# Tile finishing in a transformer layer with experts: from a fixed place in each tile step to stages placed by the list scheduler

## The chip, the cores and the metric

The kernel runs on one core of a Trainium2 chip. The metric is the device time of one execution in microseconds (us), taken as the median of several runs. A core has five engines that run beside each other, each with its own queue that it works through in order: PE (TensorE, matrix products), DVE (VectorE, elementwise work and reductions), ACT (ScalarE, activations and copies), POOL (GpSimd; here it issues the indirect transfers and takes inverse square roots) and SP (SyncE, plain transfers). An instruction that waits holds up everything behind it in its queue.

## The reference

The input x has 4 sequences of 1024 tokens with 256 channels. The first half of the layer is causal attention with 16 heads and a slope per head. The second half is a small attention over the four tokens of one position, followed by a choice of one of eight experts for each token and two layers of that expert. Cut to what matters here:

```python
h = _layernorm(x + attn_out, ln1_g, ln1_b)
flat = h.reshape(-1, C)
logits = flat @ router_w.T + router_b
probs = jax.nn.softmax(logits, axis=-1)
_, top_i = jax.lax.top_k(probs, 2)
assign = jnp.max(top_i, axis=-1)
for e in range(E):
    he = jax.nn.gelu(flat @ w1[e].T + b1[e], approximate=False)
    oe = he @ w2[e].T + b2[e]
    out = jnp.where((assign == e)[:, None], oe, out)
return _layernorm(h + moe_out, ln2_g, ln2_b)
```

So each token goes through one expert only, and x is added to what is returned.

## The kernel before

**The first 660 us** are the causal attention, with "fronts" laid between its products. A front (`front`) handles one block of 128 positions of all four sequences: normalisation, the small attention (`pr` and `sc` are scores, `pv` weighted values), the output projection `ao` with its residual, the normalisation h (root `rstd_h`, then `shift_h` and four ACT instructions that apply it), the choice of the expert (`key`, `before`, `equal`, `rank`, `hot`) and the place of each token among those of its expert (`counts_all`, `place`). It stores two rows for each token in HBM: h, and x with the last shift added.

**Tiles.** Tokens of one expert are gathered into tiles of 128. A table says which rows belong to a tile. The first table (18 tiles, 0 to 17) is made from the first six fronts, the second (20 tiles, again numbered from 0) when the last front has counted (`tabulate_rest`, lines 1228 to 1264, the product `who` at line 1314). A tile passes through these steps:

- `gather` (line 1733): an indirect transfer on POOL brings the 128 rows into one of 18 buffers `given`.
- `stages`, step 1 (line 1776): PE transposes h into the PSUM tile `t` (`mtp`; one buffer), ACT copies it (`mt`); ACT also copies the expert's first weights (line 1766).
- step 2 (line 1792): PE makes `hid`, ACT applies Gelu (`ge`, line 1801).
- step 3 (line 1811): PE makes `oe`, two tiles to a PSUM bank. With `by_product` (all of the first table, the last two of the second) PE also adds h (line 1819), else DVE does it later (line 1828) and so frees the bank early.
- finishing (`finish_tiles`): DVE takes mean and variance (lines 730, 731, 735), POOL the inverse root (`norm_root`, line 745), DVE makes the output `o` in two instructions (lines 1838 and 1841; four buffers), POOL writes a one-column clearing (`spare`, line 1848) and issues the scattered write (line 1849).

One `advance` moves each tile under way by one step, so that PE runs transposes of tile k+2, `hid` of k+1 and `oe` of k behind each other. In the old kernel `advance` begins with `finish`: finishing goes in pairs, and each tile step lets each pair under way take one more step (statistics and root; then `o`; then the output).

**The order around the change** is written out by a small list scheduler at build time (from line 2180). `threads` holds the stages of the last fronts; `free` holds when each engine is planned to be free; each stage says on which engine it is heavy and for how long; the stage that can begin first is written out next. Where PE would be free more than `TILE_HALF` (1.3 planned us) before the next stage, a tile step is written instead (`tile_step`), with the costs of `TILE`. Five tiles are held back to cover the second table. Then `late["wide"]` is set, attention's PSUM banks (`bank`, three) serve `oe` too beside its own three, and tile steps follow until nothing is left:

```python
    while experts.left():
        tile_step()
        n += 1
        if n == 8:
            check_sums()
```

`check_sums` tests whether the softmax sums are in range; its product `n_badp` and `odd` (line 2244) decide whether a general program runs behind this one.

Of the kernel before, what the change touches and what calls it, by code (L numbers as in the profile page):

```python
# [37 lines left out]
P = 128  # L38
# [30 lines left out]

TILE = (("PE", 2.6), ("DVE", 1.7), ("ACT", 1.9), ("POOL", 2.3))  # L70
TILE_HALF, LAG, COPIED, FIRST_BY, W1_THERE, LOAD_W2 = 1.3, 0.2, 1.0, 0.1, 22.0, 10.0
# [503 lines left out]
def fast_layer(ctx: ExitStack, tc: tile.TileContext, odd, x, wq, wk, wv, wp, w_in, w_out, w_r,  # L575
# [78 lines left out]
    def row(at, n=C):  # L654
        return row_sb[:, at - G1:at - G1 + n]
# [82 lines left out]
    def norm_stats(src, n, name, tag=""):  # L738
        tiles = norm_tiles(name, tag)
        for i in range(n):  # L740
            norm_one(tiles, i, src(i))
        return norm_end(tiles, n)
# [980 lines left out]
    class Tile:  # L1723
# [46 lines left out]
        def stages(self):  # L1770
# [32 lines left out]
            if late["n_oe"] % 2 == 0:  # L1803
                if late["wide"] and late["n_oe"] % 4:
                    late["oe"] = bank(f"oe_{name}").rearrange("p (k c) -> p k c", c=C)
                else:
                    late["oe"] = ps.tile([P, 2, C], F32, tag="o", name=f"oe_{name}", bufs=3)
# [14 lines left out]
    def finish_tiles(two):  # L1822

        n, name = len(two), two[0].name
        for t in two:
            if not t.by_product:
                own = t.hx[:, :C]
                nc.vector.tensor_tensor(own, own, t.v, ALU.add)
                t.v = own
        mv, rstd = norm_stats(lambda k: two[k].v, n, f"v_{name}", "_v")  # L1830
        norm_root(rstd, n)
        yield
        if experts.waiting():
            yield
        os = []
        for k, t in enumerate(two):
            o = late["work"].tile([P, C], F32, tag="o", name=f"o_{t.name}", bufs=4)
            nc.vector.scalar_tensor_tensor(  # L1838
                o, t.v, mv[:, k, 0:1], row(G2), ALU.subtract, ALU.mult
            )  # L1840
            nc.vector.scalar_tensor_tensor(  # L1841
                o, o, rstd[:, k:k + 1], t.hx[:, C:2 * C], ALU.mult, ALU.add
            )
            os.append(o)
        if experts.waiting():
            yield
        for t, o in zip(two, os):
            nc.gpsimd.memset(spare, 0.0)  # L1848
            ins = nc.gpsimd.indirect_dma_start(  # L1849
                out=out.rearrange("t n c -> (t n) c"),  # L1850
                out_offset=bass.IndirectOffsetOnAxis(ap=t.table.out_rows[:, t.j:t.j + 1], axis=0),
                in_=o, in_offset=None, bounds_check=B * T - 1, oob_is_err=False,
            )
            if late["n_out"]:
                tc.declare_no_dep(ins.ins, group="rows", reason="a token is in one tile")
            tc.add_to_no_dep_group("rows", ins.ins)
            late["n_out"] += 1

    class Experts:
# [3 lines left out]
        def __init__(self):  # L1863
            self.step, self.fetched = 0, []
            self.n_fetched = self.n_finished = 0
            self.under_way, self.done, self.finishing = [], [], []

        def fetch(self):
            self.step += 1
            if tiles_to_do and self.n_fetched - self.n_finished < len(given):  # L1870
                t = tiles_to_do.pop(0)
                t.by_product = t.table.n == 0 or len(tiles_to_do) < 2
                t.gather(given[self.n_fetched % len(given)])
                if self.n_fetched < N_OWN:
                    t.load_weights()
                self.n_fetched += 1
                self.fetched.append((t, self.step))

        def finish(self):
            for it in list(self.finishing):  # L1880
                n, stages = it
                if next(stages, self) is self:
                    self.finishing.remove(it)
                    self.n_finished += n
            n = 1 if self.done and len(self.done) + len(self.under_way) + self.waiting() < 3 else 2
            if len(self.done) >= n:
                two, self.done = self.done[:n], self.done[n:]
                self.finishing.append((len(two), finish_tiles(two)))
                next(self.finishing[-1][1])

        def waiting(self):
            return len(tiles_to_do) + len(self.fetched)

        def left(self):
            return (len(tiles_to_do) + len(self.fetched)
                    + len(self.under_way) + len(self.done) + len(self.finishing))

        def advance(self, finish=True):
            if finish:
                self.finish()  # L1900


            last = []
            if self.fetched and self.fetched[0][1] <= self.step - 3:
                t, _ = self.fetched.pop(0)
                last = [(t, t.stages())]
            if self.fetched and self.n_fetched > 2 * N_OWN + 1:
                t, _ = self.fetched[0]
                if not t.w1:
                    t.copy_w1()  # L1910
            for it in last + self.under_way[::-1]:
                t, stages = it
                if next(stages, self) is self:
                    self.under_way.remove(it)
                    self.done.append(t)
            self.under_way += last

    experts = Experts()
# [216 lines left out]
    def load_layer(sb, src):  # L2135
# [3 lines left out]
    late.update(  # L2139
        tail=tail, work=work, ps=ps_x, wide=False, n_oe=0, n_out=0, n_hid=0,  # L2140
        w1=w1_sb.rearrange("p e c f -> p (e c f)"), w2=w2_sb.rearrange("p e c f -> p (e c f)"),
# [40 lines left out]
    threads[0].ready = 9.0  # L2182
    engine_of = {"E": "DVE", "P": "DVE", "A": "ACT", "N": "ACT", "R": "POOL", "D": "PE", "d": "PE"}

# [5 lines left out]
    def take(it, at):  # L2190
# [10 lines left out]
        if it.kind == "end":  # L2201
            threads.remove(it)

    def tile_begin():
        return max(free["PE"], W1_THERE if experts.n_fetched > 2 * N_OWN else 0.0)

    def tile_step(finish=True):
        at = tile_begin()
        for on, cost in TILE:
            if on != "DVE" or experts.finishing or len(experts.done) == 2:  # L2210
                free[on] = max(free[on], at) + cost
        experts.fetch()
        experts.advance(finish)

    while threads:
        for at, what in list(of_late):
            if free["PE"] >= at:
                of_late.remove((at, what))
                what()
        at, _, it = min((begin(it) + FIRST_BY * n, n, it) for n, it in enumerate(threads))  # L2220
        if (
# [5 lines left out]
    for _ in range(HELD_BACK // 2):  # L2227
        tile_step(False)
    for _ in part.tabulate_rest():
        pass  # L2230
    late["n_oe"] += late["n_oe"] % 2
    late["wide"] = True
    for _ in range(2):
        experts.fetch()
    n = 0
    while experts.left():
        tile_step()
        n += 1
        if n == 8:
            check_sums()  # L2240
        if n == 11:
            pm = bank("n_badp")
            nc.tensor.matmul(pm[:, :1], ones_bf, n_bad, start=True, stop=True)
            nc.vector.tensor_scalar(odd, pm[:, :1], 0.0, None, ALU.not_equal)

# [88 lines left out]
```

## Time and profile before

| what | value |
|---|---|
| median of 3 runs | 841.11 us (840.54 to 841.12) |
| the profiled execution | 840.71 us |
| its span, first to last instruction | 839.0 us |
| busy: PE, DVE, ACT, POOL | 750.0, 540.9, 417.4, 251.7 us |
| mean granted clock of PE | 0.951 |
| first gather of the second table | starts at 747.71 |
| last product of PE | ends at 823.35 |
| last output on POOL | issued 830.85 to 831.89 |
| outputs, from issue to landing | 2.1 to 5.5 us, median 2.6 |

The page divides the span into 40 slices and gives each engine's busy share in tenths. A row of the timeline is: start, duration, engine, line, operation, what it writes and reads, count, and in brackets the idle time before it and what ended it. A row of groups has the count, then busy us and mean ns of one, then the idle time before the group with its releasers. A row of waits has the total, the number of waits and the longest. A row of a stretch has the stretch, its length, the busy time of PE, its weight loads, DVE, ACT and POOL (with counts), then the granted clock, the share of the DMA engines and GB/s. PE's busy time is modelled, since products overlap.

### The profile page before, as it was taken

To read this page: it belongs to the slowest core of one execution; us is meant where nothing else is said; L and a number is where in the kernel's file an instruction comes from. 1 tells how busy PE (TensorE), PEld (TensorE's weight loads), DVE (VectorE), ACT (ScalarE), POOL (GpSimd) and SP (SyncE) were. 2 spreads that over 40 slices of the span, in tenths; PEclk is the share of its full clock that TensorE was granted. 3 is DMA by queue.
4 is the path that set the end of the run, shared out by engine and by line. 5 is a ranking of instruction groups with operands and counts; after the bars stand their busy time and mean duration, and the time that the engine had idled before them with its cause. 6 is when DMAs were issued, how large, how long until landed. Compare 5 with 4: busy or idle time off the path is not lost. (4 is left out here: it accounts for less than half of the span.)

```text
span 839.0 us, 22376 instructions
## 1 busy us (share of the span) xinstructions
PE 750.0 (89%) x8917; PEld 559.0 (67%) x8917; DVE 540.9 (64%) x1300; ACT 417.4 (50%) x587; POOL 251.7 (30%) x360
## 2 busy tenths in 40 slices
PE   4898899999999999999989998998997699878972
PEld 2676667666666676666768776776766468667762
DVE  7236246339647956784777667287379869885663
ACT  1454446555455755665555555464555245333540
POOL 5443113212111312111122121121111414648885
PEclk9799989999999999999999999997999889998996
DMA  7345454524522415151634624433421652233430
GB/s 214 105 139 167 117 156 127 162 78 145 152 66 80 135 50 169 40 166 55 167 103 131 177 72 144 118 96 105 146 77 29 225 209 76 70 107 120 124 102 25
DMA packets 75219, 99.56 MB, mean 119 GB/s; under 512 B 19496, under 2 KB 58723, under 8 KB 74596
## 3 DMA queue, kind: packets, MB, share of 16 engines
q1 hardware_dynamic: 64576, 79.63, 31.7%
q0 software_dynamic: 4864, 14.16, 5.5%
q10 hardware_dynamic: 5668, 4.25, 1.7%
q8 instruction: 73, 1.20, 0.6%
q14 instruction: 38, 0.31, 0.1%
HBM read 61.55 MB, written 35.12 MB: 115 GB/s over the span
## 5 line engine op out<-in xcount | busy, mean ns | idle before, releaser
L907 ACT ACTIVATE p<-sk 128x1024 f32<-128x1024 f32 (+1 forms) x320 | 289.4, 937 | 200.7 <-PE sk L899 178.9
L917 POOL TENSOR_SCALAR_AFFINE_SELECT p<-p 128x512 f32<-128x512 f32 (+1 forms) x160 | 103.5, 650 | 458.7 <-ACT p L907 456.5
L899 PE MATMUL sk<-slots 32*128 32x128 f32 (+1 forms) x3456 | 216.5, 334 | 24.6 <-ACT p L907 21.6
L899 PEld LDWEIGHTS sk<-slots 32*128 32x128 f32 x3456 | 159.1, 189 | 82.9 <-ACT p L907 38.9
L940 PE MATMUL pv<-p,v 128*32 128x128 f32 (+1 forms) x3456 | 148.9, 322 | 0.0
L940 PEld LDWEIGHTS pv<-p,v 128*32 128x32 f32 x3456 | 99.6, 114 | 37.9 <-issue 9.2
L1519 PE MATMUL qkvp<-w_in,ut 128*128 128x264 f32 (+1 forms) x256 | 92.5, 494 | 0.2 <-DVE x L1001 0.2
L817 PE MATMUL qkp<-xt,wqk 128*128 128x256 f32 x256 | 67.2, 410 | 1.9 <-ACT xt L807 1.9
L1519 PEld LDWEIGHTS qkvp<-w_in,ut 128*128 128x128 f32 x256 | 44.4, 190 | 31.2 <-issue 25.2
L817 PEld LDWEIGHTS qkp<-xt,wqk 128*128 128x128 f32 x256 | 51.1, 206 | 13.2 <-ACT xt L807 2.3
L1526 DVE COPY qkv<-qkvp 128x264 f32<-128x264 f32 x28 | 12.1, 433 | 68.6 <-PE qkvp L1519 68.6
L1811 PE MATMUL oe<-w,ge 128*128 (+1 forms) x152 | 43.6, 412 | 13.1 <-DVE stats_v L730 6.7
L822 DVE COPY kq<-qkp 128x512 f32<-128x512 f32 x32 | 21.9, 686 | 45.6 <-PE qkp L817 45.2
L1733 POOL DMA_INDIRECT given<-rows,rows x38 | 42.8, 1126 | 20.0 <-DVE at_t L1338 10.0
L1792 PE MATMUL hid<-mt,w 128*128 128x128 f32 x304 | 45.9, 288 | 0.7 <-ACT ge L1801 0.7
L1528 ACT COPY qkv<-qkvp 128x512 f32<-128x512 f32 (+1 forms) x36 | 20.1, 562 | 51.4 <-PE qkvp L1519 51.4
L1792 PEld LDWEIGHTS hid<-mt,w 128*128 128x128 f32 x304 | 41.2, 197 | 1.9 <-ACT ge L1801 0.9
L1849 POOL DMA_INDIRECT out_dram<-o,out_rows x38 | 39.5, 1040 | 8.7 <-issue 5.9
L1008 PE MATMUL op<-wp,yc 128*128 128x256 f32 x124 | 33.1, 407 | 8.1 <-DVE yc L996 8.1
L1553 DVE TENSOR_REDUCE sc<-pr 128x64 f32<-128x1024 f32 x32 | 39.0, 1220 | 1.1
L1552 DVE TENSOR_TENSOR pr<-qkv 128x1024 f32<-128x1024 f32 x32 | 39.6, 1239 | 0.0
L1574 DVE TENSOR_TENSOR pv<-qkv,sc 128x1024 f32<-128x1024 f32 x32 | 39.2, 1225 | 0.1
(275 smaller groups left out, 976.5 us busy)
## 6 DMA issues: line engine op xcount, KB each, us to landing
slots<-k SPq DMA_DIRECT2D x128, 80.0 KB
k<-kq SPq DMA_DIRECT2D x32, 256.0 KB
v<-v SPq DMA_DIRECT2D x16, 288.0 KB
v<-v SPq DMA_DIRECT2D x4, 1152.0 KB
x<-in_x_dram SPq DMA_DIRECT2D x16, 256.0 KB
y<-yt SPq DMA_DIRECT2D x16, 256.0 KB
rows<-x SPq DMA_DIRECT2D x32, 128.0 KB
slots<-k SPq DMA_DIRECT2D x64, 64.0 KB
```

The lines of the kernel that those rows point to most:

```text
L817: nc.tensor.matmul(pm[:, k * W:(k + 1) * W], wqk[:, k, cc, half * P:(half + 1) * P], xt[:, cc], start=cc == 0, stop=cc == CC - 1,)
L899: nc.tensor.matmul(ps[h // 2][:, h % 2, width:to], kt[rows_, kb * P:(kb + 1) * P], qt[rows_, off:], start=True, stop=True,)
L907: nc.scalar.activation(pt[:, :, :width], ps[pair][:, :, :width], AF.Exp, scale=1.0 / math.sqrt(D))
L917: nc.gpsimd.affine_select(blocks, blocks, pattern=[[0, 2], [0, size], [1, P]], compare_op=ALU.is_ge, fill=0.0, base=0, channel_multiplier=-1,)
L940: nc.tensor.matmul(pv[h * S:(h + 1) * S, off:], vt[:, kb, at:at + S], pts[h // 2][:, h % 2, at_p:to], start=r == 0 and k == 0, stop=own an ...
L1519: nc.tensor.matmul(pq, ut[:, cc, t * P:(t + 1) * P], w_in_sb[:, cc, lo:hi], start=cc == 0, stop=cc == CC - 1,)
L1552: nc.vector.tensor_tensor(pr, wide(qkv[:, t, 0:C]), qkv[:, :, C:2 * C], ALU.mult)
L1574: nc.vector.tensor_tensor(pr.rearrange("p s (h d) -> p s h d", d=D), qkv[:, :, 2 * C:3 * C].rearrange("p s (h d) -> p s h d", d=D), sc[:, ...
L1733: nc.gpsimd.indirect_dma_start(out=self.hx, out_offset=None, in_=t.rows_of, in_offset=bass.IndirectOffsetOnAxis(ap=t.rows_[:, self.j:self. ...
L1792: nc.tensor.matmul(ph[:, fc], self.w1[:, cc, fc * P:(fc + 1) * P], mt[:, cc], start=cc == 0, stop=False,)
L1811: nc.tensor.matmul(self.v, ge[:, fc], self.w2[:, fc] if self.w2 else late["w2"][:, bass.ds(at + fc * C, C)], start=fc == 0, stop=False,)
L1849: ins = nc.gpsimd.indirect_dma_start(out=out.rearrange("t n c -> (t n) c"), out_offset=bass.IndirectOffsetOnAxis(ap=t.table.out_rows[:, t. ...
```

## The change

`finish_tiles` becomes a thread of the list scheduler with stages of its own: "S" (DVE, statistics of up to two tiles), "R" (POOL, one root for the group), "E" (DVE, outputs of two tiles), "R" (POOL, one clearing and two writes). Groups are of two tiles, and of four in the last stage while at least eight tiles are left; a single one at the end. The scheduler picks among fronts, the first finishing groups (with `NOT_YET` added to their time) and tile steps. `make_room` writes out finishing until a bank is planned to be free before `oe` needs one. In the last stage the `oe` pairs go round six banks, the three free ones of attention first. `check_sums` and its product come four steps later, and the product uses the transposes' PSUM tile. `by_product` is put in other words (the first 18 tiles, which are the first table's).

```diff
-TILE = (("PE", 2.6), ("DVE", 1.7), ("ACT", 1.9), ("POOL", 2.3))
+TILE = (("PE", 2.6), ("ACT", 1.9), ("POOL", 1.1))
+LATE_TILE = (("PE", 2.35), ("ACT", 1.7), ("POOL", 1.1))
+N_PRODUCT = 18
+ROOT_BY = 1.0
+NOT_YET, WHO, TABLE, GATHER = 0.4, 7.5, 10.0, 1.1
...
-                if late["wide"] and late["n_oe"] % 4:
+                late["n_wide"] += late["wide"]
+                if late["n_wide"] % 6 in (1, 2, 3):
                     late["oe"] = bank(f"oe_{name}").rearrange("p (k c) -> p k c", c=C)
...
     def finish_tiles(two):
-        for t in two:
+        stats = norm_tiles(f"v_{name}", "_v")
+        for k, t in enumerate(two):
+            if k % 2 == 0:
+                yield "S", sum(0.7 if t.by_product else 1.1 for t in two[k:k + 2])
             if not t.by_product:
                 own = t.hx[:, :C]
                 nc.vector.tensor_tensor(own, own, t.v, ALU.add)
                 t.v = own
-        mv, rstd = norm_stats(lambda k: two[k].v, n, f"v_{name}", "_v")
+                experts.n_released += 1
+            norm_one(stats, k, t.v)
+        mv, rstd = norm_end(stats, n)
+        yield "R", 0.75
         norm_root(rstd, n)
-        yield
-        if experts.waiting():
-            yield
...
+        for at in range(0, n, 2):
+            some = two[at:at + 2]
+            yield "E", len(some) * 1.0
...
+            yield "R", 0.2 + len(some) * 1.05
             nc.gpsimd.memset(spare, 0.0)
-            ins = nc.gpsimd.indirect_dma_start(
+            for t, o in zip(some, os):
+                ins = nc.gpsimd.indirect_dma_start(
...
+        def make_room(self):
+            if late["n_oe"] % 2 == 0:
+                while late["n_oe"] - self.n_released >= (12 if late["wide"] else 6):
+                    it = self.finishing[0]
+                    take(it, begin(it))
...
+        def next_finishing(self):
+            return self.finishing[:2] + [it for it in self.finishing[2:4] if it.kind == "S"]
...
             for it in last + self.under_way[::-1]:
                 t, stages = it
+                self.make_room()
...
+            n = 1 if rest < 3 else 4 if late["wide"] and rest >= 8 else 2
+            while len(self.done) >= n:
+                two, self.done = self.done[:n], self.done[n:]
+                self.finishing.append(Running(finish_tiles(two)))
+                self.finishing[-1].ready = free["PE"] + LAG
...
-        at, _, it = min((begin(it) + FIRST_BY * n, n, it) for n, it in enumerate(threads))
+        at, _, it = next_of(
+            [(it, FIRST_BY * n) for n, it in enumerate(threads)]
+            + [(it, NOT_YET) for it in experts.next_finishing()]
+        )
...
-    late["n_oe"] += late["n_oe"] % 2
     late["wide"] = True
...
     while experts.left():
-        tile_step()
-        n += 1
-        if n == 8:
-            check_sums()
-        if n == 11:
-            pm = bank("n_badp")
+        at, _, it = next_of(
+            [(it, -ROOT_BY * (it.kind == "R" and it.cost < 1)) for it in experts.next_finishing()]
+            or [(never, 0.0)]
+        )
+        if at > tile_begin() and experts.to_step():
+            tile_step()
+            n += 1
+            if n == 12:
+                check_sums()
+            if n == 15:
+                pm = ps_x.tile([P, CC, P], F32, tag="t", name="n_badp")[:, 0]
...
+        else:
+            take(it, begin(it))
```

## The prediction

> **What bounds the kernel now.** All times are us from the span's start in the profiled execution: it took 840.71, its span is 839.0, and the median of the three runs is 841.11, 0.4 above. About 0.2% (1.7 us) is what a measurement here can tell from no change.
>
> I read first the page's slices, to see where an engine other than TensorE is loaded:
>
> ```profile
> PE   4898899999999999999989998998997699878972
> ...
> POOL 5443113212111312111122121121111414648885
> ```
>
> Attention keeps PE at 9 for most of the span and the change does not touch it. Only in the last five slices (from 734) does POOL rise to 8. So I took the groups of POOL from the first gather of the second table (747.71) to the last output:
>
> ```profile
> L1849 POOL DMA_INDIRECT out_dram<-o,out_rows x32 | 32.8, 1026 | 7.6 <-issue 4.8 <-DVE o L1841 2.3 <-DVE stats_v L730 0.4
> L1733 POOL DMA_INDIRECT given<-rows,rows x20 | 22.1, 1107 | 14.8 <-DVE at_t L1338 10.0 <-issue 3.4 <-PE hid L1796 1.1
> L745 POOL TENSOR_TENSOR rstd_v<-rstd_v,minus_half 128x2 f32<-128x2 f32 (+1 forms) x15 | 11.1, 737 | 2.3 <-DVE rstd_v L735 2.0
> L1848 POOL MEMSET spare<- 128x1 f32 x32 | 3.7, 116 | 0.1
> ```
>
> Busy 32.8+22.1+11.1+3.7 = 69.7 of the 84.2 from 747.71 to 831.89. Of the idle, 10.0 lies before 747.71 and only 2.3+2.0 = 4.3 is a wait for DVE; the rest are gaps of 0.2 to 0.3 between queued instructions. **From 747.71 POOL is full.** The timeline shows one pair of it, and the same six repeat every 6.2 (795.96 to 802.16):
>
> ```profile
> 795.96 0.73 POOL L745 TENSOR_TENSOR rstd_v<-rstd_v,minus_half 128x2 f32<-128x2 f32 x1
> ...
> 796.88 1.28 POOL L1733 DMA_INDIRECT given<-rows,rows  x1 [0.19 <-issue]
> ...
> 798.46 1.02 POOL L1849 DMA_INDIRECT out_dram<-o,out_rows  x1 [0.19 <-issue]
> ...
> 799.79 1.00 POOL L1849 DMA_INDIRECT out_dram<-o,out_rows  x1 [0.19 <-issue]
> ```
>
> PE needs only 2 x 2.3 = 4.6 a pair there (802.22 to 804.5 is one tile) and waits for banks that a late finish frees. PE's and POOL's waits by who ended them (total, times, longest):
>
> ```profile
> PE oe L1811 <- DVE stats_v L730: 6.7, 2, 3.5
> PE oe L1811 <- DVE given L1828: 6.3, 5, 1.6
> PE mtp L1776 <- ACT mt L1778: 2.2, 1, 2.2
> ```
> ```profile
> POOL given L1733 <- DVE at_t L1338: 10.0, 1, 10.0
> ```
>
> So PE's 13.0 of bank waits are an effect of the POOL queue, not the bound. The end of the kernel is (when the second table is there, call it T = 747.71) + (POOL's queue from T) + the 7.1 behind the last output (831.89 to 839.0), which the change leaves.
>
> **Part 1: T, by DVE's order.** T ends DVE's chain of the last front. Before, finishing stands inside it:
>
> ```profile
> 704.08 0.48 DVE L1838 SCALAR_TENSOR_TENSOR o<-oe,mv_v,rows 128x256 f32<-128x256 f32 x1
> ...
> 704.20 0.42 ACT L1563 ACTIVATE sc<-sc 128x256 f32<-128x256 f32 x1 [0.22 <-DVE sc L1561]
> ...
> 707.27 0.19 DVE L1538 TENSOR_TENSOR u<-qkv,told 128x32 f32<-128x32 f32 x1
> ```
>
> The softmax is back from ACT at 704.62 but DVE finishes tiles until 707.27. In the order built from the changed kernel:
> - The statistics of tiles 0,1 (699.33 to 700.61, 1.28) go behind the last score: the chain to the exponential is 1.28 earlier. They and those of 2,3 (1.28) now lie in its shadow: the last score step ends at 702.9 (704.16 - 1.28), 702.9 + 2.56 = 705.4 against 707.27, gain 1.9.
> - The finishing at 708.93 to 712.11 (3.2) leaves the front of `pv`: gain 5.05 in all, `pv` at 707.1 against 712.11. ACT's exponential moves ahead of one Gelu with its table load; PE's tile 5 then ends at 707.9 instead of 706.4, which costs nothing, since PE waits for `pv` to 709.1 anyway.
> - The outputs of 0,1 lie in DVE's wait for `ao` (2.3 idle). Those of 2,3 stand between two `ao` (+1.9) but 4,5's and the statistics of 6,7 (726.31 to 729.49) shrink to the 1.28 of 4,5, beside POOL's root: shift_h at 724.6 against 729.49, gain 4.9.
> - The 3.2 between `equal` and its product (731.81 to 734.98) goes: `hot` at 729.1 against 737.01, gain 7.9. The outputs of 4,5 (1.9) come back behind it, so DVE is ready for `rank` at 733.6.
>
> What is late next is **PE**: tiles 8 and 9 moved behind `ao`, so four tiles (2.75 each, 727.54 to 730.27) stand between `ao` and `counts_all`. `ao` ends at 719.75 (724.80 - 5.05); two tiles to 725.2; the third needs ACT's copy, which queues behind the four normalisations released by shift_h (before, 729.49 to 732.59, 3.1): 727.7. That is a stall of 2.5. The trace has one of 2.15 there (730.44 to 732.59), and the clock behind it:
>
> ```profile
> 732.60:736.80 4.20, 4.20 (x17) 3.63 (x18) 3.89 (x14) 1.99 (x5) 3.48 (x6) 0.60 0.42 133
> ```
>
> (last three: granted clock, DMA share, GB/s). A tile took 4.6 there (732.59 to 737.20), not 2.75; after the 1.6 stalls it took 2.3 as ever. I charge 4.6: 727.7+4.6+2.75 = 735.1 for `counts_all`, `rank` 0.7 later at 735.8 against 739.52. T follows 8.19 behind as before: **744.0, gain 3.7**. With no clock loss PE is ready at 733.2, `rank` at 733.9 and T at 742.1; with no gain T stays 747.7.
>
> [...]
>
> **What moves but costs nothing.** PE has the same instructions in both (the same 20 tiles add h by a product). SP's order is unchanged; its store of the last normalised rows starts 8 earlier with `hot` (before, 739.66). On POOL the gathers of tiles 12 and 13 now stand behind the outputs of 2,3 and the front's root (to 724.4): tile 12's lands near 729 (1.0 to issue, 3.5 median to land) and is wanted behind `counts_all`. POOL stood idle for 10.0 before T, and by the same intervals it has all first-table gathers and the outputs of 4,5 done at 736.5. The check of the sums (2.0 on DVE) comes four steps later, at T+22.2 to T+24.2, where DVE waits for a root anyway (the next ends at T+25.5).
>
> **Part 2: POOL's queue from T.** 20 gathers and 32 outputs stay. Roots: seven of at most two columns (0.74) and five of four (1.03, as in the front's 1.01 and 1.04) = 10.3, was 11.1. Clearings 17 x 0.116 = 2.0, was 3.7. Busy 32.8+22.1+10.3+2.0 = 67.2. Gaps: 17 outputs behind a clearing x 0.185 = 3.1; 15 outputs directly behind an output, no row; gathers 13 x 0.30 + 6 x 0.19 = 5.0. For output behind output the nearest row is gather behind gather (749.03 to 750.34): 0.30. **A dropped clearing (0.116+0.19) is then replaced by an equal gap: sharing saves nothing.** Low end: no gap, -4.5. High end: the slowest gather of this tail, 2.04 at 715.95 beside DVE's 1024-wide products, 1.0 more each, +15. I take 0.30: 67.2+3.1+4.5+5.0 = 79.8.
>
> Does POOL ever wait? I laid its queue out by these intervals against DVE and PE:
> - Five gathers stand before the root of 6,7 now; DVE waits for it to T+7.2 with the outputs of 6 to 9 and the statistics of 12 to 15 queued behind. Nobody needs those banks: three free banks and three held ones let PE run tiles 12 to 17 (to T+14.6) unblocked.
> - Later roots find their statistics 4 or more early, e.g. 12 to 15 ready T+13.7, root T+19.1; tiles 6 to 9 ready T+43.5, root T+47.6.
> - `odd` (L2244) now shares the transposes' bank, so PE's next tile waits for DVE's read: 0.4 once, with E of 14,15 behind it on DVE; their outputs start 0.5 or more later.
> - PE is done near T+62; the last 17 are POOL emptying its queue. The four `o` buffers: an output lands in 2.6 (median), two pairs take 5.3. Margins in the last 25 are about 1.
>
> So the 4.3 of waits at the end goes too: 84.2 to 79.8, **gain 4.4**.
>
> **Sum.** 840.71 - 3.7 - 4.4 = 832.6; at the median's scale (+0.4) **833.0**.
>
> **Rivals.**
> - *A, the forecast*, 0.52: 828.5 to 836.5, i.e. T between 742.1 and 746, waits on POOL up to 1.5.
> - *B, half of it*, 0.20: PE's four tiles or DVE in order eat one part. If T stays: 841.1-4.4 = 836.7; if POOL's waits stay: 841.1-3.7 = 837.4. For: 1 us margins. Against: the walk above.
> - *C, more*, 0.10: no clock loss (1.9) and no gap between outputs (4.5): 833.0-6.4 = 826.6. For: the 1.0 of a DMA is the same behind a clearing and behind a gather.
> - *D, slower*, 0.10: back-to-back outputs without a clearing run longer. Place: 15 pairs on a full POOL. It decides from 8.1/15 = 0.54 more than the 0.30 each; at the 1.0 of the slowest gather, 833.0+15 = 848. For: no row shows the sequence, and the one DMA row far above 1.3 (2.04) shows that POOL's issue can stretch. Against: gathers run back to back at 1.31, and DVE's 1024-wide products are over by T.
> - *E, it does not do it*, 0.08: groups of four make POOL wait for whole groups, about 8 in sum, 841.
>
> Faster by over 0.2%: A, B and C, 0.82. Within: E, 0.08. Slower: D, 0.10. Range: from C's 826 to B's 839; E and D stay out.
>
> **What would show it.** Right: first gather of the second table at 742 to 746; POOL's DVE waits after it under 1.5; last output about 80 after it; PE's bank waits (13.0) near zero and PE ending some 17 before POOL; a PE stall over 2 at the transposes with the clock near 0.6 behind it. Wrong: an output behind an output starting later than 0.5 after it or taking over 1.3; T at 747; POOL idle on `rstd_v` or `o`.

## The result, and the profile after

The first comparison gave 843.66 us (median of 20 runs, 837.7 to 849.36) against 839.84 for the kernel before (20 runs): a ratio of 1.0048, 95% interval [1.0028, 1.0069]. The forecast was 833.0 with a range of 826 to 839 and a chance of 0.82 for faster. The time is outside the range and on the other side.

The same kernel, unchanged, was then measured three more times beside the kernel before, and the answers fall into two kinds:

| run of the changed kernel | median, us | kernel before, us | ratio, 95% interval |
|---|---|---|---|
| first comparison | 843.66 | 839.84 | 1.0048 [1.0028, 1.0069] |
| r_after | 833.34 | 839.44 | 0.9925 [0.9896, 0.9955] |
| r_after2 | 833.21 | 839.14 | 0.9930 [0.9903, 0.9956] |
| r_after3 | 846.28 | 840.95 | 1.0062 [1.0033, 1.0091] |

So the document has two questions: where the first comparison lost what the forecast promised, and why two of four comparisons didn't lose it. r_after, r_after2 and r_after3 ran on three different chips; which one the first comparison ran on isn't known.

The profile of the first comparison's execution (845.16, span 843.5), page, slices of PE and POOL:

```profile
PE   4998989998999999999999998998998698889960
...
POOL 5533123212120311111221121121121321667565
```

POOL's 8 in the last slices has become 5 to 7: it isn't full any more. Its groups from 738 on, as columns count, busy us and mean ns, then idle time ahead and who ended it:

```profile
L1860 POOL DMA_INDIRECT out_dram<-o,out_rows x32 | 33.3, 1041 | 13.5 <-DVE o L1852 6.8 <-issue 5.3 <-DVE o L1849 0.6
L1737 POOL DMA_INDIRECT given<-rows,rows x20 | 21.7, 1087 | 19.6 <-issue 12.1 <-DVE at_t L1342 6.8 <-PE mtp L1780 0.3
L749 POOL TENSOR_TENSOR rstd_v<-rstd_v,minus_half 128x2 f32<-128x2 f32 (+2 forms) x12 | 10.3, 859 | 0.5 <-issue 0.3
L1858 POOL MEMSET spare<- 128x1 f32 x17 | 2.0, 119 | 0.0
```

Busy is 33.3+21.7+10.3+2.0 = 67.3, and the forecast said 67.2. The idle ahead of outputs and gathers is what differs. The timeline shows that it is two holes:

```profile
778.25 1.01 POOL L1860 DMA_INDIRECT out_dram<-o,out_rows  x1 [0.30 <-issue]
787.20 1.06 POOL L1737 DMA_INDIRECT given<-rows,rows  x1 [7.95 <-issue]
...
815.05 0.11 POOL L1858 MEMSET spare<- 128x1 f32 x1
821.16 1.03 POOL L1860 DMA_INDIRECT out_dram<-o,out_rows  x1 [5.99 <-DVE o L1852]
```

From T = 742.59 to the end of the last output at 836.32 are 93.7 us; 93.7 - 7.95 - 5.99 = 79.8, the forecast's queue to the digit. "issue" at the first hole means that the profile sees nobody; the program does: this gather goes into the buffer of tile 14 of the first table, which DVE gives back when it makes that tile's output. DVE's timeline at that moment, and at the second hole:

```profile
780.01 0.17 DVE L739 TENSOR_SCALAR rstd_v<-mv_v 128x4 f32<-128x4 f32 x1
785.35 0.16 DVE L2283 TENSOR_SCALAR odd<-n_badp 128x1 int32<-128x1 f32 x1 [5.18 <-PE n_badp L2282]
785.43 0.47 DVE L1849 SCALAR_TENSOR_TENSOR o<-oe,mv_v,rows 128x256 f32<-128x256 f32 x1
785.94 0.48 DVE L1852 SCALAR_TENSOR_TENSOR o<-o,rstd_v,given 128x256 f32<-128x256 f32 x1
...
819.05 0.43 DVE L734 BATCH_NORM_STATS2 stats_v<-oe 128x6 f32<-128x256 f32 x1 [4.57 <-PE oe L1825]
```

The outputs of tiles 14 and 15 (785.43 on) stand behind `odd`, `odd` waits 5.18 for PE, and POOL waits for them. The second hole is the same kind: DVE takes the statistics of tile 18 ahead of the outputs of 10 to 15 and waits 4.57 for PE's tile, which is late. Both holes come from a **late PE**. It ends at 819.0, T+76.4; the forecast said T+62.

Why is it late? Not by banks: no `oe` waits for DVE any more (13.0 before), and none of PE's waits from 738 on is for a gather. PE's and then ACT's rows around the first stall:

```profile
746.20 0.38 PE L1780 MATMUL mtp<-ident,given 128*128 128x128 f32 x2
...
747.42 0.22 PE L1800 MATMUL hid<-chosen,b_bf 128*128 128x128 bf16 x1
...
751.76 0.49 PE L1796 MATMUL hid<-mt,w 128*128 128x128 f32 x2 [2.44 <-ACT ge L1805]
```
```profile
748.42 0.37 ACT L1782 COPY mt<-mtp 128x256 f32<-128x256 f32 x1 [2.37 <-PE hid L1800]
751.32 0.38 ACT L1805 ACTIVATE ge<-hid 128x256 f32<-128x256 f32 x1 [2.53 <-remote]
```

By PE's record `mtp` is done at 746.58, but ACT copies it at 748.42; `hid` is done at 747.64, but ACT's Gelu starts at 751.32, and PE's next `hid` needs that Gelu. The same tile in r_after2:

```profile
746.86 0.38 PE L1780 MATMUL mtp<-ident,given 128*128 128x128 f32 x2
...
748.08 0.22 PE L1800 MATMUL hid<-chosen,b_bf 128*128 128x128 bf16 x1
```
```profile
747.33 0.37 ACT L1782 COPY mt<-mtp 128x256 f32<-128x256 f32 x1 [0.62 <-PE mtp L1780]
748.39 0.38 ACT L1805 ACTIVATE ge<-hid 128x256 f32<-128x256 f32 x1 [0.69 <-PE hid L1800]
```

Here each reader starts 0.1 behind PE. I paired every copy `mt` and every Gelu `ge` that ACT starts behind a wait from 730 on with the end of the matmul that it reads, in all traces of the study. Five of them, with the median and the late ones (over 0.6 us) and their sum:

| trace | waits | median, us | late | sum, us | T+ at PE's end | queue from T |
|---|---|---|---|---|---|---|
| before | 51 | 0.10 | 0 | 0 | 75.6 | 84.2 |
| changed, r_after | 54 | 0.10 | 0 | 0 | 62.7 | 81.5 |
| changed, r_after2 | 53 | 0.10 | 0 | 0 | 62.7 | 81.3 |
| changed, first comparison | 46 | 0.10 | 15 | 27.0 | 76.4 | 93.7 |
| changed, r_after3 | 46 | 0.10 | 15 | 27.3 | 74.1 | 91.4 |

That is what tells the two kinds apart: **signals in time** or **late signals** from PE. The late ones lie between 734 and 817, several at the same place in both traces (T+5.8 and T+5.9; T+8.7 and T+8.9; T+69.2 and T+69.0). Two other things go with them in each trace of that kind: the trace holds 13,518 to 13,544 records of semaphore changes instead of some 14,256, and most of the missing ones are landings of POOL's transfers (572 fewer of them in the first comparison's 13,526 records than in the 14,283 of the kernel before), so that the list of transfers has no median time to landing. That list in r_after2 (the last number is the median), and then in r_after3:

```profile
out_dram<-o,out_rows POOLq DMA_INDIRECT x32, 2.5
given<-rows,rows POOLq DMA_INDIRECT x20, 3.7
```
```profile
out_dram<-o,out_rows POOLq DMA_INDIRECT x31
given<-rows,rows POOLq DMA_INDIRECT x20
```

PE loses the time in two ways. The stretch from T to PE's end, in the first comparison and then in r_after2 (after the length comes PE's busy time; the granted clock is the last number but two):

```profile
742.59:819.02 76.43, 67.48 (x432) 57.26 (x430) 47.73 (x144) 30.60 (x70) 53.95 (x63) 0.93 0.36 106
```
```profile
743.25:805.95 62.70, 61.36 (x432) 53.91 (x430) 46.12 (x139) 31.30 (x70) 51.51 (x60) 1.00 0.41 125
```

Of the 13.7 us by which PE is later, 7.6 are idle time and 6.1 are the same 432 matmul records taking longer, at a lower granted clock (0.93 against 1.00).

### The profile page after: what moved, and what is told of

Same layout as the page of the kernel before. It is cut to its first block, busy times and chain, and to the rows that moved or that the text cites. A ratio compares the mean times of both kernels' runs of the same rounds, so it can differ in the third digit from the quotient of the medians.

```text
span 843.5 us, 22366 instructions
## 1 busy us (share of the span) xinstructions
PE 752.4 (89%) x8917; PEld 561.7 (67%) x8917; DVE 541.4 (64%) x1295; ACT 416.5 (49%) x587; POOL 244.9 (29%) x337
## 5 line engine op out<-in xcount | busy, mean ns | idle before, releaser
L903 PE MATMUL sk<-slots 32*128 32x128 f32 (+1 forms) x3456 | 215.7, 335 | 21.8 <-ACT p L911 20.9
L1796 PE MATMUL hid<-mt,w 128*128 128x128 f32 x304 | 48.7, 299 | 12.4 <-ACT ge L1805 8.9
```

Of the source, the lines that this page charges most:

```text
L903: nc.tensor.matmul(ps[h // 2][:, h % 2, width:to], kt[rows_, kb * P:(kb + 1) * P], qt[rows_, off:], start=True, stop=True,)
L1796: nc.tensor.matmul(ph[:, fc], self.w1[:, cc, fc * P:(fc + 1) * P], mt[:, cc], start=cc == 0, stop=False,)
```

## The experiments

**The kernel as it is, again: r_after, r_after2, r_after3.** No edit.

> The changed kernel as it is, for a second profile. In the first one POOL stands idle twice behind the first gather of the second table: 7.95 us ahead of the gather at 787.20 and 5.99 us ahead of the output at 821.16; together 13.94, and 79.8 (the forecast's queue) + 13.9 is the 93.7 from T to the last output. Theory: the first hole is built into the order (the finishing of tiles 14 and 15 stands on DVE behind the comparison that writes odd, and that waits 5.2 us for PE), so it is there again within 1 us of its length. The second needs PE to be late with the last two tiles; PE's 3.4 us wait for a Gelu at 812 may be an accident of one execution. If both holes come again at the same places with the same lengths, both are built into the order; if the second is gone, the span is 4 to 6 us shorter (about 838).

Measured: 833.34, span 833.5. Both holes are gone: the gather into tile 14's buffer has a gap of 0.71, the largest later gap is 1.20. `odd` still waits, 2.7 instead of 5.2. So the first theory (the first hole is built into the order) fell: the order only makes the hole possible, and a late PE makes it.

> The changed kernel as it is, once more, since the first comparison (843.66 us, ratio 1.0048) and the run r_after (833.34, ratio 0.9925) disagree by 10 us about one and the same kernel. In r_after's profile TensorE does the tiles behind 738.8 in 68.5 us without a stall over 0.6, and in the first one it takes 83.2, with six places where its signals come 1.5 to 5 us late. Theory (the difference lies with TensorE in an execution, not in the order): a time near 833 where the tiles run undisturbed, near 843 where they come late; a value between (836 to 840) would say that the first comparison held both kinds.

Measured: 833.21, no late signal. DVE's wait for `odd`, and the hole behind it:

```profile
DVE odd L2283 <- PE n_badp L2282: 3.1, 1, 3.1
```
```profile
780.63 1.06 POOL L1737 DMA_INDIRECT given<-rows,rows  x1 [1.12 <-issue]
```

> The changed kernel as it is, a third time, to learn whether the 843.66 of the first comparison comes again. It stood at 833.34 and 833.21 in the two comparisons since. If the first one was an accident of that comparison: 832 to 835. If there are two kinds of executions of this kernel, each holding for a whole comparison: either 832 to 835 or 841 to 846, and in the second case TensorE's signals come 1.5 to 5 us late at several places behind 730 in the profile.

Measured: 846.28, the second kind. The hole ahead of the same gather is 10.55 (at 792.00), `odd` waits 5.44. The second hole does not come again (1.10 ahead of the same output), so it is not part of the kind. The span is 11.4 above r_after2's, and the parts add up: T, measured from a matmul that the change leaves in place, comes 3.0 later, the queue is 10.1 longer, and that matmul itself comes 1.6 earlier.

**odd at the end: e1_odd_last, e1b_odd_last, e1c_odd_last.**

```diff
-            if n == 15:
-                pm = ps_x.tile([P, CC, P], F32, tag="t", name="n_badp")[:, 0]
-                nc.tensor.matmul(pm[:, :1], ones_bf, n_bad, start=True, stop=True)
-                nc.vector.tensor_scalar(odd, pm[:, :1], 0.0, None, ALU.not_equal)
         else:
             take(it, begin(it))
+    pm = ps_x.tile([P, CC, P], F32, tag="t", name="n_badp")[:, 0]
+    nc.tensor.matmul(pm[:, :1], ones_bf, n_bad, start=True, stop=True)
+    nc.vector.tensor_scalar(odd, pm[:, :1], 0.0, None, ALU.not_equal)
```

> The matmul n_badp and the comparison that writes odd are moved from behind step 15 to the end of the loop; nothing else changes. Theory (the comparison holds up DVE): DVE runs on at 780.2 instead of 785.4, tile 14 gives its buffer back 5.2 us earlier, the hole ahead of the gather shrinks from 7.95 to about 2.5, and the time falls by 5 us against the changed kernel (838 to 839); by up to 11 (832 to 833) if the second hole goes with it. Rival (POOL is not what counts, PE's late tiles are): the hole moves to the outputs at the end and the time is within 1 us of the changed kernel (843 to 844).

> Again the kernel with n_badp and odd at the end of the loop, in the hope of a comparison of the second kind. In comparisons of the first kind (r_after, r_after2) ScalarE's waits for TensorE end 0.1 us behind the matmul, and the kernel as changed is at 0.9925 and 0.993 of the kernel before; in the second kind (the first comparison, r_after3, e6_clear_each) 15 or 16 of some 45 of these waits end 0.6 to 4 us late, 27 to 32 us in sum, and the ratio is 1.005 to 1.008. Theory: where the signals are late, the comparison that writes odd costs 5 us of the loss, so the ratio is 0.998 to 1.002 there; where they are in time, 0.990 as before. Rival (any place of odd has the same loss): 1.005 to 1.008 there.

> odd at the end alone. First kind: 0.990 again. Second kind: theory, 0.998 to 1.002, 4 to 6 us below the kernel as changed (1.005 to 1.008); rival, 1.005 to 1.008.

Measured: 832.51, ratio 0.9904 [0.9872, 0.9937]; 831.15, 0.9902 [0.9865, 0.9939]; 830.93, 0.9920 [0.9888, 0.9953]. All three fell in comparisons with signals in time, where the expected loss isn't there to be saved. The changed kernel itself ran beside only the first: by the medians e1_odd_last is 0.8 below r_after, and the intervals overlap. What odd's place costs where signals are late naturally stays unmeasured.

**Groups of two: e2_pairs, e2b_pairs.**

```diff
-            n = 1 if rest < 3 else 4 if late["wide"] and rest >= 8 else 2
+            n = 1 if rest < 3 else 2
```

> Groups of two instead of four in the last stage; everything else of the change stays, odd behind step 15 too. Theory (the comparison's place is to blame): POOL gets 5 more roots (some 2 to 2.5 us of queue) and the wait for odd stays, so the time is 0 to 3 us above the changed kernel. Rival (groups of four hold buffers and outputs back, since the second half of a group is finished only behind the outputs of the first): tiles 14 and 15 are finished some 10 us earlier, the hole ahead of the gather is gone, and the time falls by 4 us or more, to under 840.

> Again groups of two instead of four, for the same reason. Theory (groups of four put the finishing of tiles 14 and 15 far back, which costs only where TensorE's signals are late): 0.995 to 1.000 in a comparison of the second kind, 0.9935 in one of the first. Rival (odd behind step 15 is enough to stop DVE): 1.004 to 1.009 in the second kind.

Measured, signals in time both times: 833.7, 0.9935 [0.9909, 0.9961], and 833.18, 0.9925 [0.9899, 0.9951]. In the trace of e2_pairs, 17 roots take 12.5 instead of 12 taking 10.1 in r_after, and the queue from T is 83.4 instead of 81.5: the five saved roots are there, as the theory says, but 1.9 us is less than the medians can show. The rival (groups of four hold buffers back) finds nothing with signals in time; with late signals groups of two were not measured.

**PE delayed: d1_late_after, d2_late_before, d3_late_odd_last.** Matmuls that nobody reads, in the last loop of each kernel; d3 has odd at the end as well.

```diff
             n += 1
+            if n in (4, 9, 14):
+                pm = ps_x.tile([P, CC, P], F32, tag="t", name=f"late_{n}")[:, 0]
+                for _ in range(36):
+                    nc.tensor.matmul(pm, ident, ident, start=True, stop=True)
```

> The changed kernel with TensorE made late on purpose: 36 matmuls of 128 columns that nobody reads (some 4 us at the full clock) behind each of the steps 4, 9 and 14 of the last loop; the work of the layer is unchanged. Theory (the new order has no reserve against a late TensorE, since odd, the statistics of the last tiles and the gathers stand on DVE and POOL behind it): the 12 us of delay bring the holes of the first profile back and the time rises by 6 to 12 us, to 840 to 845. Rival (TensorE ends 17 us ahead of POOL's last output, so 12 us are hidden): at most 2 us above the run without delay.

> The kernel before with the same three delays behind steps 4, 9 and 14 of its last loop. Theory (its TensorE waits 13 us for banks in any case and so swallows a delay): 1 to 4 us above the kernel before (841 to 843), less than the changed kernel loses. Rival (a late TensorE costs both kernels the same): the rise is within 2 us of that of the changed kernel.

> The changed kernel with n_badp and odd at the end of the loop and the same three delays. Theory (the comparison that writes odd is the place where DVE waits for a late TensorE): 4 to 6 us below the changed kernel with the delays. Rival (any late tile stops the queues, odd is one place among several): within 2 us of it.

Each delay took 8.2, not 4 (in the trace of d1 the 36 four-byte matmuls are 72 instructions, 0.11 apart; one of the delays of d2 took 8.55), 24.6 in sum. In one comparison, with signals in time and 833.21 for the kernel without delay: changed 859.67, ratio 1.0239 [1.0195, 1.0283]; before 860.9, 1.0261 [1.022, 1.0302]; with odd at the end 856.16, 1.0189 [1.0143, 1.0235]. So the changed kernel lost 26.5 (6 to 12 was expected for delays of 12), the kernel before 21.8, and odd at the end 23.7 against e1_odd_last's 832.51 of another comparison. The first hole of the first comparison is there again, larger; the second is not (1.19), and a new one of 4.49 stands ahead of a root. d1_late_after, POOL and DVE:

```profile
807.40 1.06 POOL L1737 DMA_INDIRECT given<-rows,rows  x1 [22.06 <-issue]
```
```profile
805.55 0.16 DVE L2287 TENSOR_SCALAR odd<-n_badp 128x1 int32<-128x1 f32 x1 [13.13 <-PE n_badp L2286]
```

It is the same gather and the same comparison on DVE. That a late PE makes this hole is thereby shown, at a lateness larger than the natural one. The rest fell on both sides: 24.6 of delay against 17 of lead is hidden in neither kernel (the kernel before was to lose 1 to 4), and moving odd away saves 3.5 by the medians (the intervals overlap), less than the theory's 4 to 6 and more than its rival's 2. The trace of d3_late_odd_last shows why it is so little:

```profile
795.36 1.07 POOL L1737 DMA_INDIRECT given<-rows,rows  x1 [8.75 <-PE hid L1800]
```
```profile
786.78 0.42 DVE L1836 TENSOR_TENSOR given<-given,oe 128x256 f32<-128x256 f32 x1 [5.06 <-PE oe L1825]
```

The same gather still has a hole of 8.75, since DVE now waits for PE (5.06, then 2.53) with the sums and statistics of other tiles, which also stand ahead of tile 14's output. POOL's holes of over 0.8 come to 24.1 in sum, against 27.7 in d1_late_after. So `odd` is one place among several where a late PE stops the queues.

**Half the delay: d4_late_half, d5_before_half.** 18 matmuls instead of 36, some 4.2 each and 12.5 in sum.

> The changed kernel with delays half as long: 18 matmuls instead of 36 behind each of the steps 4, 9 and 14. The long ones took 8.2 us each by the profile (a matmul of four-byte numbers is two instructions, 0.11 us each), so these take 4.1, 12.3 in sum, near the 14.7 by which TensorE is later in the first profile than in that of the second comparison. Theory (TensorE's lateness and the holes behind it make the first comparison's 10 us): 8 to 13 us above the run without delay, 841 to 846. Rival (12.3 us vanish in the 17 us that TensorE is ahead, and the first comparison was slow for another reason): 833 to 837.

> The kernel before with the same half delays. The long ones cost it 21.8 us (the changed kernel 26.5) of the 24.6 that the profile shows them to take. Theory (it swallows what its TensorE would have waited for banks): 6 to 10 us above the kernel before, 3 to 5 less than the changed kernel loses. Rival: the same loss as the changed kernel, within 2 us.

Measured in the comparison of r_after3, with late signals: 863.4, 1.0277 [1.0243, 1.0312], and 851.66, 1.0147 [1.0108, 1.0185]. On top of the natural lateness (846.28) the changed kernel lost 17.1 for 12.5 of delay, more than both theories allowed; the kernel before lost 10.7 (6 to 10 was expected). d4's trace has 14 late signals of 47 (27.7 us), d5's 4 of 48 (3.1). So the kernel before met the same chip with hardly any late signal, though its trace lacks as many records (13,544).

**A clearing ahead of each output: e6_clear_each.**

```diff
-            nc.gpsimd.memset(spare, 0.0)
             for t, o in zip(some, os):
+                nc.gpsimd.memset(spare, 0.0)
```

> The changed kernel with a clearing ahead of every output instead of every pair. The forecast says that sharing saves nothing, as 0.12 of clearing and 0.19 of gap stand where else a gap of 0.30 is: within 1 us of the changed kernel (832 to 835). Rival (15 clearings at 0.30 are saved): 4.5 us above it, 837 to 839.

Measured in the same comparison, with late signals (16 of 46): 847.52, 1.0080 [1.0044, 1.0116], 1.2 above r_after3. The rival's 4.5 would be 1.0116, the very end of the interval; the theory's nothing lies inside. The trace says it more plainly: without its holes of over 0.8 POOL's queue takes 80.1, against 79.7 in r_after3.

**The banks in turn: e8_banks_alt.** The old order of the banks, with the limit that it needs.

```diff
-                while late["n_oe"] - self.n_released >= (12 if late["wide"] else 6):
+                while late["n_oe"] - self.n_released >= ({1: 8, 3: 10}.get(late["n_wide"], 12) if late["wide"] else 6):
...
-                if late["n_wide"] % 6 in (1, 2, 3):
+                if late["wide"] and late["n_wide"] % 2:
```

> The changed kernel with the banks of the two pools taken in turn, as the kernel before does, instead of the three free ones first; the limit on tiles not given back is tightened at the turn to match. Theory: the three free banks spare TensorE a wait for DVE at the turn, which it can afford as it ends 17 us ahead of POOL; so within 2 us of the changed kernel in either kind (0.992 or 1.006). Rival (the early lead is what the ratio of 0.993 comes from): 3 us or more above it, and in the second kind fewer late signals.

Measured, signals in time: 835.98, 0.9972 [0.9948, 0.9996], against 0.9902 and 0.9925 of e1b_odd_last and e2b_pairs beside it; the changed kernel itself was not in this comparison. The theory fell. PE and POOL:

```profile
746.90 2.08 PE L1816 MATMUL oe<-w,ge 128*128 x4 [2.95 <-DVE o L1849]
```
```profile
781.00 1.06 POOL L1737 DMA_INDIRECT given<-rows,rows  x1 [5.10 <-issue]
```

PE waits 2.95 for a bank and runs slowly behind it (granted clock 0.62 from 747 to 751): that tile takes 7.22 instead of 2.74, 4.5 later. Thirty-four us on, the gather into tile 14's buffer has a hole of 5.10 (1.12 in r_after2), and the queue from T is 86.3 instead of 81.3. This is the clearest single experiment: PE late by 4.5 once, with no late signal (0 of 52), makes the first hole and leaves a gain of 0.003 where r_after and r_after2 had 0.007 to 0.008 in their comparisons (the intervals overlap a little).

**Two halves between PE and ACT: e9_two_th, e9b_two_th; with odd at the end: e10_both.** The bank of the transposes and that of `hid` hold two tiles each.

```diff
+            k = late["n_mt"] % 2
+            late["n_mt"] += 1
+            if "t" not in late:
+                late["t"] = ps.tile([P, 2, CC, P], F32, tag="t", name="mtp")
+                late["h"] = ps.tile([P, 2, CC, P], F32, tag="h", name="hid")
-            pt = ps.tile([P, CC, P], F32, tag="t", name=f"mtp_{name}")
+            pt = late["t"][:, k]
...
-            ph = ps.tile([P, CC, P], F32, tag="h", name=f"hid_{name}")
+            ph = late["h"][:, k]
...
-                pm = ps_x.tile([P, CC, P], F32, tag="t", name="n_badp")[:, 0]
+                pm = late["t"][:, 0, 0]
```

> The changed kernel with two halves each for the transposed tile and the hidden units in PSUM, taken in turn, so that TensorE doesn't wait for ScalarE to empty the last tile's half before it fills the next. Theory (a late signal stops TensorE since these are single): in a comparison of the second kind TensorE loses 5 us or less instead of 14 and the ratio falls to 0.995 to 1.000; in the first kind 0.992 to 0.994, since TensorE isn't the bound there. Rival (the lateness is TensorE's own, its matmuls really end late): no change in the second kind, 1.005 to 1.008.

> Two halves alone. First kind: 0.990 again. Second kind: theory, 0.995 to 1.000; rival (matmuls that really end late), 1.005 to 1.008.

> Both mends at once: n_badp and odd at the end of the loop, and two halves each for the transposed tile and the hidden units. In a comparison of the first kind (signals in time): 0.988 to 0.991 of the kernel before, as each alone (0.990). In the second kind: theory (the two places where a late signal stops a queue), 0.993 to 0.998; rival (lateness costs whatever the order), 1.003 or more.

Measured, all with signals in time: 831.72, 0.9898 [0.9863, 0.9933]; 831.82, 0.9909 [0.9878, 0.9941]; both together 832.12, 0.9914 [0.9885, 0.9943]. These and odd at the end stand 6 to 9 us under the kernel before and are not told apart from each other, nor from what the changed kernel gains with signals in time (6 us). Whether they hold with late signals could not be seen: no comparison of that kind came up again.

## Why the prediction was wrong, point by point

- **The bound, T + POOL's queue + the tail**: right in both kinds. Without its holes of over 0.8 us the queue is 79.3 to 80.3 in all four traces of the changed kernel, against 79.8, and 7.1 lie behind the last output in each.
- **Part 1, T**: right in direction; the size differs by execution. Measured from a bias matmul that the change leaves in place (689.60 before, 690.36 in r_after2, 688.47 in the first comparison, 688.81 in r_after3), T came 58.1 behind it before, and 52.9, 54.1 and 55.9 after: a gain of 5.2 (5.0 in r_after), 4.0 and 2.3, against 3.7. The stall at the transposes came as forecast (2.11 to 2.12 in all four against 2.5). The clock loss behind it, charged with 1.9, came in r_after3 (0.58) and not in the other three (1.00 in the first comparison and in r_after2). Windows of r_after2 and, behind the stall, of r_after3, the last three columns granted clock, DMA share, GB/s:

```profile
727.00:731.00 4.00, 2.21 (x16) 1.99 (x17) 3.69 (x12) 3.19 (x9) 3.20 (x4) 1.00 0.46 131
731.00:735.00 4.00, 4.00 (x37) 3.55 (x36) 3.60 (x7) 1.97 (x4) 3.39 (x3) 1.00 0.63 200
```
```profile
726.74:730.74 4.00, 4.00 (x16) 3.45 (x17) 3.79 (x9) 2.00 (x5) 3.09 (x4) 0.58 0.44 131
```

  So the same gap at the same place was followed by a low clock in one trace of four, and the 1.9 rested on a single trace. Behind longer gaps the clock was low: 2.44 idle before 751.76 in the first comparison, then 0.60; 2.95 in e8_banks_alt, then 0.62.
- **Part 2, the pieces of the queue**: right. Busy 67.3 against 67.2; an output behind an output starts 0.30 behind it and takes about 1.0; a root of four columns 1.04 to 1.22. Rival D, which was to be the slower case, is refuted by the same rows. (The "same six" of the kernel before that repeat every 6.2 are seven: a pair takes two gathers there, at 796.88 and 801.09. No sum used the six.)
- **Part 2, "Does POOL ever wait?"**: this is the step that failed. The walk let PE run tiles at 2.3 to 2.75 with its results at the readers at once, ended PE near T+62, and from that put the outputs of 14 and 15 at "0.5 or more later" and the last margins at "about 1". A wait of DVE for PE at `odd` was not in it: its "0.4 once" is PE's wait for DVE there. With signals in time the rest holds: PE ends at T+62.7, `odd` holds DVE for 2.7 to 3.1, POOL's holes are 0.7 to 1.2 each, the queue is 81.3 to 81.5. In the first comparison PE ended at T+76.4, `odd` held DVE for 5.2, and POOL stood for 7.95 and 5.99. The walk also saw only one end of the chain: that tile 14's outputs would be late, not that a gather waits for that tile's buffer with all of POOL's queue behind it. The 17 by which PE was to end ahead of POOL were no reserve against this either: in the four traces of the changed kernel and in those with delays (d1, d4) the last output ends 17.2 to 18.8 behind PE's end, with PE's end anywhere from T+62.7 to T+93.4. The time follows a late PE almost one for one.
- **The sum**: 833.0 was met by the two comparisons with signals in time (833.34, 833.21), and missed by 10.7 and 13.3 in the others. That it was met so closely is luck: T gained 1.5 more than forecast in r_after2, and the queue 1.5 less (84.2 to 81.3 is 2.9, not 4.4). The kernel before stood at 839.1 to 841.0 in the four.
- **The rivals** had no case of a late PE, though the text itself named the margin of 1 us that made the result depend on PE. E's 8 us of waits are near the size measured, but its mechanism wasn't seen: with signals in time groups of two give the same time as groups of four. With late signals groups of two were not measured.

**What stays open.** Shown: a late PE produces the first hole at the same gather (d1_late_after, d4_late_half, e8_banks_alt), and in the traces of the two comparisons that the changed kernel lost, 15 of 46 of ACT's waits end late behind the recorded end of PE's result (up to 3.96 us in the first comparison's; 27.0 and 27.3 in sum). Not shown: why the results come late there, and why the kernel before, with 4 late signals in its one trace of that kind (d5_before_half), is nearly spared. The three runs of the kernel before that stand ahead of the prediction are the first three of its 20 in the first comparison; the trace that goes with them has 14,283 records and no late signal, but which chip it was taken on isn't known. Three chips gave signals in time (one of them twice) and one gave late signals, which suggests that the chip decides, but five comparisons don't prove it.

No run here tells a late signal from a matmul that really ended late: what the traces show is the recorded end of a matmul and the start of its reader, 0.10 apart in the median and up to 3.96 in the first comparison's.

Some 5% of the records of semaphore changes are missing in the traces with late signals (13,518 to 13,544 instead of some 14,256). Whether that goes with the lateness isn't shown: d5_before_half lacks as many (13,544) with hardly a late signal (4 of 48), and no run here separates recording from execution.

## What to carry to other kernels

When a static order takes waits out, write beside each engine's lead what stands behind the first instruction that reads its result: here PE ended 17 us ahead of POOL, but DVE read PE's newest results in mid-stream (a flag for a fallback, the sums and statistics of the next tiles), and a gather on POOL waited behind them, so the lead was no reserve. Moving one such reader, the flag, to the end of its queue saved 3.5 of the 26.5 us that a delayed PE cost, by medians whose intervals overlap, and nothing measurable where PE was in time; the other readers stayed. And compare a kernel with small gains on more than one chip before the sign is believed: here the same kernel was at 0.993 and at 1.006.

## What the runs showed of the hardware

- In the five traces of the table ACT starts 0.10 us (median) behind the recorded end of the matmul that it reads. It came up to 3.96 behind it in the first comparison's trace and 4.86 in d4_late_half's, over 0.6 behind it 14 to 16 times in some 46 in each of the four traces of the changed kernel with late signals (the first comparison's, r_after3, d4_late_half, e6_clear_each), 4 times in 48 in d5_before_half, and never in the other traces (0 of 50 to 55 in each).
- In the first comparison's trace 10 of the 15 late waits end within 0.06 us of a landing of one of POOL's transfers, where a moment taken at random is some 0.36 away in the median. In r_after3 it is 6 of 15 and in e6_clear_each 3 of 16, where chance alone would give about 2. Whether one causes the other isn't known.
- PE gaps of 2.1 to 3.0 us behind 690 were followed by a lower clock in some cases and not in others: over all 20 traces, the 4 us behind them had a granted clock of 0.57 to 0.63 for 9 of 25, and 1.00 for the other 16. Of the 20 gaps of 2.11 to 2.15 at the transposes four were followed by it (2.15 before, 2.12 in r_after3, but not 2.12 in r_after2), of the five from 2.42 to 2.95 all (2.44 in the first comparison, 2.95 in e8_banks_alt).
- On POOL an indirect transfer issued behind another starts 0.30 behind it whichever way it goes, and a clearing in between (0.12, then 0.19) takes the place of that gap; with a clearing ahead of every output POOL's queue without its holes was 80.1, against 79.3 to 80.3 (e6_clear_each).
